# Issue order of one 1 MB output copy against the held weight loads in a top-2 expert layer

## The chip, the cores and the metric

One NeuronCore of a Trainium2 chip runs the whole program. The metric is the device time of one execution in microseconds (us). It was measured three times for the kernel before; the median is quoted. One further execution was recorded by the hardware profiler, and all rows of a profile come from that one.

In this document PE is the tensor engine, DVE the vector engine, ACT the scalar engine, POOL the GpSimd engine and SP the sync engine. SP computes nothing here: it issues DMAs, one after the other, in the order of the program. A q behind a name (SPq, POOLq) marks the instructions of that engine's sequencer.

## The reference

A residual layer with eight experts of three matrices each, of which every token uses two:

```python
var = jnp.mean(x * x, axis=-1, keepdims=True)
xn = rms_w * (x * jax.lax.rsqrt(var + EPS))
gate = xn @ wg_W + wg_b + (genre_embed @ gg_W + gg_b)
gate_w = jax.nn.softmax(gate, axis=-1)
topk_w, topk_i = jax.lax.top_k(gate_w, TOP_K)            # TOP_K = 2 of E = 8
cw = jnp.sum(jax.nn.one_hot(topk_i, E, dtype=x.dtype) * topk_w[..., None], axis=-2)
h1 = jax.nn.relu(jnp.einsum('bsh,ehm->bsem', x, W1) + b1)      # 256 -> 512
h2 = jax.nn.relu(jnp.einsum('bsem,emn->bsen', h1, W2) + b2)    # 512 -> 512
out_e = jnp.einsum('bsen,enh->bseh', h2, W3) + b3              # 512 -> 256
return jnp.einsum('bseh,bse->bsh', out_e, cw)
```

The result is `x + ref(x)`. `x` is 64 x 64 x 256 in float32, that is 4096 tokens of 1 KB each. An expert's W1 and W3 have 512 KB each and its W2 has 1 MB, so the weights make 16 MB and x makes 4 MB.

## The kernel before

The kernel does not compute all experts for all tokens. It computes the gate, sorts the 8192 (token, expert) pairs into tiles of 128 tokens that share an expert, gathers the rows of a tile, runs the three layers on them, and adds the weighted rows onto the output.

**Two parts.** Partition p holds the tokens 32p to 32p+31. The first NA = 8 columns of each partition (1024 tokens) are "the first part": their gate is computed first (`first_part`, L404), so that a first tile for each of the eight experts can start early. Tiles 0 to 7 hold rows of these tokens alone. The other 24 columns are routed while tiles 0 to 6 already run (`rest`, L556), and all later tiles come from that second table.

**The output** is built by addition. Plain copies put x into the output in DRAM, and each tile's weighted rows are then added to it by an indirect DMA (`give`, L862). The copies are `fills`. The first one (L509) covers the first 8 columns: 128 runs of 8 KB, 1 MB from DRAM to DRAM. Four more (L929) of 768 KB each follow during tiles 3 to 6. Each add waits for the add before it, the very first one waits for `fills[0]`, and the first add of the second table waits for the other fills.

**The order of the DMAs.** Everything is under a manual schedule, so each engine runs its instructions in program order. On SP this is: loads of x (L154), the bias vectors (L444 and L445), W1 and W2 of expert 0 (L395), and then what `other_loads` (L496) issues. Its first DMA is W3 of expert 0, and it carries an added dependence on `fetches[0]`, the gather of tile 0's 128 rows (`gather(0)`, L983). It is called the hold below. Since SP works in order, nothing behind the hold is issued until those rows have landed. Behind it come W1 of expert 1, b3 of experts 0 and 1, W2 and W3 of expert 1, the copy of the first columns (L509), the weights of expert 2, the rest of b3 and the weights of experts 3 to 7, in total some 15 MB besides the copy.

POOL issues the indirect DMAs: the gathers of rows into `xg` (L712), the gathers of the routing weights into `cg` (L712), the adds (L868), and it writes the routing weights to DRAM (L378).

PE transposes tile 0's rows (`transpose_x`, L767), ACT copies them to SBUF (L768), and then layer 1 (L831), layer 2 (L842) and layer 3 (L858) follow for each tile. ACT applies bias and relu (L834, L845), and DVE scales and adds the bias of the third layer (L867).

Of the kernel before, what the change touches and what calls it, by code (L numbers as in the profile page):

```python
# [21 lines left out]
def kernel(  # L22
# [17 lines left out]
    nc = tc.nc  # L40
# [13 lines left out]
    NA = 8  # L54
# [15 lines left out]
    xr = xrows.rearrange("(p i) h -> p i h", p=P)  # L70
    our = orows.rearrange("(p i) h -> p i h", p=P)
# [314 lines left out]
    fills, loads, fetches = [], [], []  # L386

    def load_weights(e, parts=(0, 1, 2)):
        for k in parts:
            dst, src = (  # L390
                (w1a[:, e], W1[e].rearrange("(p c) m -> p c m", c=HC)),
                (w2a[:, e], W2[e].rearrange("(c p) n -> p c n", p=P)),
                (w3a[:, e], W3[e].rearrange("(c p) h -> p c h", p=P)),
            )[k]
            loads.append(nc.sync.dma_start(dst, src))  # L395
# [100 lines left out]
    def other_loads():  # L496


        load_weights(0, (2,))
        tc.add_manual_dep(  # L500
            loads[2].ins,
            fetches[0].ins.name,
            mybir.DependencyInfo(mybir.DependencyClass.Sync, mybir.DependencyReason.DATA),
            reason="the first tile's rows go first",
        )
        load_weights(1, (0,))
        nc.sync.dma_start(b3_sb[:, 0:2], b3[0:2].unsqueeze(0).to_broadcast([P, 2, H]))
        load_weights(1, (1, 2))
        fills.append(nc.sync.dma_start(our[:, 0:NA, :], xr[:, 0:NA, :]))  # L509
        load_weights(2)  # L510
        nc.sync.dma_start(b3_sb[:, 2:E], b3[2:E].unsqueeze(0).to_broadcast([P, E - 2, H]))
        for e in range(3, E):
            load_weights(e)
# [467 lines left out]
    with tc.manual_schedule():  # L981
        first_part()
        gather(0)  # L983
        other_loads()
        gather(1)
        second_part()
# [73 lines left out]
```

## Time and profile before

| what | value |
|---|---|
| three executions | 511.5 to 511.92 us, median 511.85 us |
| the profiled execution | 513.2 us, of which its span is 511.4 us |
| granted PE clock, mean | 0.995 |
| PE busy | 495.6 us, 97% of the span |
| PE weight loads busy | 445.4 us, 87% |
| DVE / ACT / POOL busy | 239.2 / 167.3 / 288.9 us |
| HBM read / written | 42.80 / 20.71 MB |

The span is the stretch from the first to the last instruction in the profile. The page gives the busy time of each engine, the span in 40 slices, the DMA queues and the costliest groups of instructions. The trace behind it can be asked for the instructions of one engine in order of time, for what each engine waited for, and for the busy share of engines and DMA in any stretch. In such answers the first number of a timeline row is the start in us from the start of the span, the second the duration; square brackets tell how long the engine had been idle before the row and what ended that. A row of windows gives busy time and number of instructions of each engine, then the granted clock, the mean busy share of the 16 DMA engines, and the GB/s moved.

### The profile page before, as it was taken

The numbers are of one execution on the slowest core, as the hardware profiler recorded it, in microseconds if no ns is written. First come the engines' busy times: TensorE is split into PE (matmuls) and PEld (weight loads), VectorE is DVE, ScalarE is ACT, GpSimd is POOL, SyncE is SP. The second block draws the span as 40 slices with busy tenths as digits, with TensorE's granted clock in tenths as the row PEclk, the third lists the DMA queues.
The fourth block names the chain that finished last, engine by engine and source line by source line (L and its number), as shares of the span: only waits on it lengthen the run. The fifth ranks groups of instructions, "written<-read, shape, count | busy, mean of one in ns | idle before, by whom it ended". The sixth has DMA issues, their size and how long they took to land. (4 is left out here: it accounts for less than half of the span.)

```text
span 511.4 us, 8669 instructions
## 1 busy us (share of the span) xinstructions
PE 495.6 (97%) x2840; PEld 445.4 (87%) x2840; DVE 239.2 (47%) x587; ACT 167.3 (33%) x394; POOL 288.9 (56%) x229
## 2 busy tenths in 40 slices
PE   7899999999999999999999999999999999999992
PEld 6679999888888888888888888888888889999991
DVE  5895977244444334334333444443333335655550
ACT  5734444322222222222222222222222222444340
POOL 3455517766666656655556556666565545764621
PEclk9999999999999999999999999999999999999997
DMA  8699996454433343333433344433343333434201
GB/s 326 203 378 393 388 382 204 88 104 80 88 72 79 72 79 77 73 68 75 83 75 76 81 82 84 79 69 80 77 82 64 61 64 53 93 61 77 42 3 23
DMA packets 68257, 59.26 MB, mean 116 GB/s; under 512 B 39615, under 2 KB 59298, under 8 KB 67812
## 3 DMA queue, kind: packets, MB, share of 16 engines
q1 hardware_dynamic: 52608, 41.21, 24.6%
q0 software_dynamic: 15232, 17.34, 21.0%
q8 instruction: 25, 0.41, 0.3%
q14 instruction: 36, 0.29, 0.2%
q10 hardware_dynamic: 356, 0.01, 0.0%
HBM read 42.80 MB, written 20.71 MB: 124 GB/s over the span
## 5 line engine op out<-in xcount | busy, mean ns | idle before, releaser
L842 PE MATMUL pb<-hid,big 128*128 128x256 f32 (+1 forms) x1120 | 210.8, 346 | 0.0
L842 PEld LDWEIGHTS pb<-hid,big 128*128 128x128 f32 x1120 | 187.0, 191 | 20.4
L868 POOL DMA_INDIRECT out_dram<-y,idxR x59 | 97.8, 1658 | 127.9 <-issue 73.1
L845 ACT ACTIVATE hid<-pb,bb 128x256 f32<-128x256 f32 (+1 forms) x140 | 61.5, 440 | 245.7 <-PE pb L842 233.0
L797 DVE COPY big<-w2a 128x2048 f32 x35 | 44.7, 1278 | 160.4 <-PE pb L842 154.9
L831 PE MATMUL pb<-xT,big 128*128 128x256 f32 (+1 forms) x560 | 108.2, 346 | 0.0
L858 PE MATMUL pb<-big,hid 128*128 128x256 f32 x472 | 107.6, 379 | 0.0
L831 PEld LDWEIGHTS pb<-xT,big 128*128 128x128 f32 x560 | 93.5, 191 | 9.9
L858 PEld LDWEIGHTS pb<-big,hid 128*128 128x128 f32 x472 | 88.8, 190 | 11.6
L712 POOL DMA_INDIRECT big<-in_x_dram,idxR x59 | 78.8, 1336 | 20.7 <-issue 17.1
L712 POOL DMA_INDIRECT cg<-cwdR,idxR x59 | 69.0, 1169 | 18.0 <-issue 18.0
L834 ACT ACTIVATE hid<-pb,bb 128x256 f32<-128x256 f32 (+1 forms) x140 | 61.5, 440 | 40.9 <-PE pb L831 26.9
L867 DVE SCALAR_TENSOR_TENSOR y<-pb,cw,bc 128x256 f32<-128x256 f32 x59 | 28.5, 483 | 46.6 <-issue 26.2
L792 DVE COPY big<-w1a 128x1024 f32 x35 | 24.3, 695 | 25.5 <-PE pb L831 22.9
L842 PEld LDWEIGHTS pb<-hid,w2a 128*128 128x128 f32 x256 | 29.9, 192 | 2.3 <-issue 2.0
L842 PE MATMUL pb<-hid,w2a 128*128 128x128 f32 x256 | 30.7, 277 | 0.9 <-issue 0.9
L868 POOL DMA_INDIRECT out_dram<-y,idxA x8 | 15.7, 1963 | 25.1 <-DVE denB L370 7.8
L801 DVE COPY big<-w3a 128x1024 f32 x35 | 25.8, 737 | 2.8 <-issue 2.8
L816 DVE TENSOR_SCALAR bc<-b_sb,cw 128x256 f32 x59 | 22.9, 389 | 2.1
L756 DVE STREAM_TRANSPOSE xT<-gTs 128x256 f32<-128x256 f32 x57 | 22.5, 424 | 0.7 <-DMA gTs<-scr 0.7
L845 ACT ACTIVATE hid<-pb,vT 128x128 f32<-128x128 f32 x32 | 11.4, 367 | 25.3 <-PE pb L842 23.7
L831 PE MATMUL pb<-xT,w1a 128*128 128x128 f32 x128 | 16.0, 278 | 0.0
(224 smaller groups left out, 252.2 us busy)
## 6 DMA issues: line engine op xcount, KB each, us to landing
w2a<-in_L_cond_W_dram SPq DMA_DIRECT2D x8, 1024.0 KB
scr<-big SPq DMA_DIRECT2D x57, 128.0 KB
gTs<-scr SPq DMA_DIRECT2D x228, 32.0 KB
w1a<-in_L_cond_W_dram SPq DMA_DIRECT2D x8, 512.0 KB
w3a<-in_L_cond_W_dram SPq DMA_DIRECT2D x8, 512.0 KB
out_dram<-in_x_dram SPq DMA_DIRECT2D x4, 768.0 KB
big<-in_x_dram SPq DMA_DIRECT2D x4, 512.0 KB
big<-in_x_dram SPq DMA_DIRECT2D x2, 1024.0 KB
```

The source lines that it names most:

```text
L712: return nc.gpsimd.indirect_dma_start(out=dst, out_offset=None, in_=src, in_offset=bass.IndirectOffsetOnAxis(ap=index(b), axis=0), bounds_ ...
L792: V.tensor_copy(st1, w1a[:, e].rearrange("p e c m -> p (e c) m"))
L797: V.tensor_copy(st2, w2a[:, ex[u]].rearrange("p e c m -> p (e c) m"))
L801: V.tensor_copy(st3, w3a[:, ex[u]].rearrange("p e c m -> p (e c) m"))
L816: V.tensor_scalar(bc, b3e, cw, None, ALU.mult)
L831: nc.tensor.matmul(ph, lhsT=w1[:, c, ts(m, P)], rhs=cols[:, c, :], start=(c == 0), stop=(c == HC - 1))
L834: nc.scalar.activation(hids[:, 0, m, 0 : w * BT], ph, AF.Relu, bias=bb[:, 0, m : m + 1])
L842: nc.tensor.matmul(ph, lhsT=w2[:, m, ts(n, P)], rhs=hids[:, 0, m, 0 : w * BT], start=(m == 0), stop=(m == MC - 1))
L845: nc.scalar.activation(hids[:, 1, n, 0 : w * BT], ph, AF.Relu, bias=bb[:, 1, n : n + 1])
L858: nc.tensor.matmul(po, lhsT=hids[:, 1, n, ts(k, BT)], rhs=w3[:, n, :], start=(n == 0), stop=(n == MC - 1))
L867: V.scalar_tensor_tensor(y, sums(b), cw, bc, ALU.mult, ALU.add)
L868: add = nc.gpsimd.indirect_dma_start(out=orows, out_offset=bass.IndirectOffsetOnAxis(ap=index(b), axis=0), in_=y, in_offset=None, bounds_c ...
```

## The change

The copy of the first eight columns is issued as the first DMA of `other_loads`, ahead of the hold, and no longer behind W3 of expert 1. Nothing else differs: the same DMAs with the same sizes are issued, on the same queue, and the dependences are the same.

```diff
     def other_loads():
 
 
+        fills.append(nc.sync.dma_start(our[:, 0:NA, :], xr[:, 0:NA, :]))
         load_weights(0, (2,))
         tc.add_manual_dep(
             loads[2].ins,
...
         load_weights(1, (0,))
         nc.sync.dma_start(b3_sb[:, 0:2], b3[0:2].unsqueeze(0).to_broadcast([P, 2, H]))
         load_weights(1, (1, 2))
-        fills.append(nc.sync.dma_start(our[:, 0:NA, :], xr[:, 0:NA, :]))
         load_weights(2)
         nc.sync.dma_start(b3_sb[:, 2:E], b3[2:E].unsqueeze(0).to_broadcast([P, E - 2, H]))
```

## The prediction

> **What bounds the kernel now.** I read the busy times of the page first, then the list of what PE waited for after the first 20 us, because PE is the engine that is never free.
>
> ```profile
> PE 495.6 (97%) x2840; PEld 445.4 (87%) x2840; DVE 239.2 (47%) x587; ACT 167.3 (33%) x394; POOL 288.9 (56%) x229
> DMA  8699996454433343333433344433343333434201
> ```
> ```profile
> PE pb L842 <- issue: 0.9, 1, 0.9
> PE pb L767 <- DMA xg<-in_x_dram,idxA: 0.7, 1, 0.7
> ```
>
> PE is at 97%. From 20 to 505 us it has two idle moments. In one (0.7 us, at 22.00) it waits for the rows of tile 0, in the other (0.9 us, at 36.77) for no weight: layer 2 of tile 1 needs ACT's last relu of layer 1, which ends at 37.67. PE never waits for a weight load. So a PE instruction that starts later at 22 us ends the kernel later by as much, and a weight that lands earlier is worth nothing. The DMA row shows full rings (9) only in the slices up to 77 us, and a dip in the second. The timelines of SP, PE and POOL show what happens in the dip:
>
> ```profile
> 11.55 0.43 SPq L395 DMA_DIRECT2D w2a<-in_L_cond_W_dram  x1
> 21.98 0.37 SPq L395 DMA_DIRECT2D w3a<-in_L_cond_W_dram  x1
> 24.95 0.68 SPq L509 DMA_DIRECT2D out_dram<-in_x_dram  x1
> ```
> ```profile
> 20.22 1.06 PE L214 MATMUL pb<-hid,wg_sb 128*32 128x512 f32 x8
> 22.00 0.50 PE L767 MATMUL pb<-ident,xg 128*128 128x128 f32 x2 [0.72 <-DMA xg<-in_x_dram,idxA]
> ```
> ```profile
> 19.04 1.12 POOL L712 DMA_INDIRECT xg<-in_x_dram,idxA  x1 [6.12 <-DVE denA L369]
> 23.17 0.63 POOL L378 DMA_DIRECT2D cwdA<-cw8A  x1 [0.29 <-POOL cw8A L377]
> 30.07 1.06 POOL L712 DMA_INDIRECT cg<-cwdA,idxA  x1 [3.62 <-DMA cwdA<-cw8A]
> ```
>
> SP stands at the hold from 12 to 21.98. The gather of tile 0 leaves POOL at 19.04+1.12 = 20.16, and PE has its rows at 22.00: 1.84 us. What the rings do meanwhile is in the windows (the last two numbers: DMA share, GB/s):
>
> ```profile
> 17.00:18.00 1.00, 0.99 (x13) 0.98 (x14) 0.88 (x3) 0.90 (x2) 0.00 (x0) 1.00 0.64 242
> 18.00:19.00 1.00, 1.00 (x12) 0.83 (x11) 0.54 (x5) 0.00 (x0) 0.00 (x0) 1.00 0.07 18
> 19.00:20.00 1.00, 1.00 (x9) 0.93 (x9) 0.90 (x6) 0.59 (x1) 0.96 (x1) 1.00 0.00 0
> 20.00:21.00 1.00, 1.00 (x11) 0.21 (x9) 0.93 (x5) 0.58 (x1) 0.69 (x2) 1.00 0.18 41
> 33.00:34.00 1.00, 1.00 (x11) 1.00 (x10) 0.90 (x6) 0.40 (x2) 0.83 (x1) 1.00 1.02 425
> 34.00:35.00 1.00, 1.00 (x7) 0.90 (x7) 0.83 (x6) 0.06 (x1) 0.87 (x1) 1.00 1.04 438
> ```
>
> The loads ahead of the hold run out between 17 and 18. In windows of a quarter us the rings carry nothing from 18.5 to 20.75, where the packets of the gather begin; they end at 21.5.
>
> **The change part by part.** It removes and adds no instruction. It moves one SP issue (0.68 us by its row) from 24.95 to about 12.0, where SP would only wait, so that issue costs nothing and the hold still ends with the gather. Behind the hold five DMAs keep their place, and everything from W1 of expert 2 on is issued without the 0.7 us and without the copy's data in the rings. If that cover (the hold) were gone, the 0.68 us would fall on SP, which PE does not wait for.
>
> How long does the copy take in the rings? The packet records show 8 KB packets, which only this transfer has in that stretch, from 32.6 to 35.4, of 309 ns each, eight to an engine: 8 x 0.309 = 2.47 us. The windows above agree: 1.05 MB at 425 to 438 GB/s are 2.4 to 2.5 us. How much room is there? Until 20.75 the free share is 0.36 + 0.93 + 1.00 + 0.75 = 3.04 us of all 16 engines. So on the mean engine the copy ends some 0.5 us before the gather's first packet. The last packets of the loads are over just after 18.0, so the slowest engine ends the copy at about 18.1 + 2.47 = 20.6, still 0.15 us before it. Two instruction fetches stand in the same hole (packets of 0.47 us at 17.9 and 1.07 us at 18.3); if one of them lands on a late engine, that engine ends at up to 21.6.
>
> What is late then is the gather of tile 0, and with it PE's transposes at 22.00, ACT's copy at 22.54, layer 1 at 22.97 and all of PE behind them, one for one. Call this delay d. It is bounded from both sides. Below: zero, because the index of the gather comes from DVE at 18.8 and nothing in the change touches that. Above: the same trace shows what a POOL transfer pays with the rings full. The write of the routing weights leaves POOL at 23.17+0.63 = 23.80 and its waiter goes on at 30.07, 6.3 us, where the gather in empty rings had 1.84. Fully loaded rings would therefore cost up to 4.4 us more. I take d = 0.2 us, near the empty case, because by the sum the copy has gone on nearly all engines.
>
> Here two rules of the Trainium skill speak. "DMA: Bandwidth & Descriptors", in the section on the anatomy of one DMA, fits a transfer as about 2.0 us fixed plus its bytes at 436 GB/s. For the copy that makes 2.0 + 2.4 = 4.4 us, ending at 17.6 + 4.4 = 22.0 instead of 20.1, and would put it right on the gather (an estimate of d = 22.0 - 20.75 = 1.25, which gives 513.1). The packet rows show 2.47 us back to back in the rings, since the fixed part is latency and occupies no engine, so I use the row. The same page, on queues and rings, says that an engine takes turns between its queues packet by packet. Then a leftover of the copy would cost each of the gather's two packets per engine one packet of 0.31 us, d = 0.6 at most (512.45). The row of 6.3 us does not look like fair turns, so the trace leaves more room than the rule. I use the rule for the middle and the row for the tail.
>
> What is gained? The weights and b3 behind the copy's old place land about 2.5 us earlier. W1 of expert 2 is needed at 40.7 and its bytes pass at about 36, so it was early already: nothing. The last fills and the first gathers of the second table meet freer rings near 80 us, and PE does not wait there either: nothing. The add that waits for this copy starts at 42.23 after a DVE wait: nothing. One thing could be positive. ACT's relus of layer 1 of tile 1 run 1 us apart (33.69, 35.13, 35.87, 37.30) instead of the 0.45 of tile 0, just while the copy's packets pass, and PE's 0.95 us of idleness follows from it. If the copy caused that, up to 0.95 us comes back. The fills of 768 KB later, also from DRAM to DRAM, show no such gap, so I count 0.
>
> **The sum.** Profiled execution: span 511.4 + 0.2 = 511.6, and with the 1.8 us around it 513.2 + 0.2 = 513.4. The median of the runs is 1.35 us under the profiled execution; the same difference on it gives 511.85 + 0.2 = 512.05, told as 512.0.
>
> **The rivals.**
> (1) Hidden, as summed: 512.0, chance 0.67. For it: the 3.04 us of room against 2.47. Against it: the margin is only 0.15 to 0.5 us, and the copy writes DRAM as well.
> (2) Slower: the copy's tail is still in the rings when POOL hands over the gather. It decides from the point where an engine still holds copy packets after about 20.7. Place: tile 0's rows at 22.00. Price: an engine with the long fetch ends at 21.6; if the gather's first packet then still needs the 0.6 us that it needs in empty rings (20.16 to 20.75), it starts at 22.2, so d is 22.2 - 20.75 = 1.45, hence 513.3; with the full queueing of the 6.3 us row d = 4.4, 516.3. Chance of d over 1 us: 0.25.
> (3) Faster: the copy was what spread ACT's relus at 33 to 37 us. The gain is 0.95 us of PE's idleness and no more, since PE has no other; 510.9, with a little more if the timed runs lose more there. For it: the coincidence in time. Against it: the lag begins before the copy's first packet, and the timed runs are 1.35 us under the profiled one, so they may not have it at all. Chance of more than 0.2%: 0.08.
> (4) The copy is hidden in both places, so that only noise moves. This lies inside case (1).
>
> **How the numbers follow.** 0.2% of 511.85 is 1.0 us, about what a measurement of this kernel can tell from no change. Within it lies case (1), with d up to 1.0, and most of a recovered 0.95: 0.67. Slower is case (2), 0.25, faster what is left of case (3), 0.08. The range reaches from the full recovery, 510.9, to the 513.3 of case (2); beyond it I leave about 0.07 below and 0.12 above, for longer queueing.
>
> **What would show it.** Right: the copy's SP row at about 12.0; DMA shares near 1 in the windows 17 to 20 and falling before 21; SP's hold ending within 0.3 us of 21.98; PE's L767 row near 22.0; later SP rows some 2.5 us earlier once rings limit them. Case (2): L767 at 23 or later, and its idle time, ended by the DMA of xg, up from 0.72 by as much as the end moves. Case (3): the four relus of L834 for tile 1 some 0.45 us apart and no idle row of L842 at 37.7. I am wrong if the gather, though handed to nearly empty rings, lands over 1 us late, or if PE waits somewhere new behind 38 us.

## The result and the profile after

In 20 executions of each kernel the changed one has a median of 512.8 us, the one before 511.93 us. The ratio is 1.0018, with a 95% interval from 1.001 to 1.0025: slower by 0.9 us, between 0.5 and 1.3. A second comparison, in the last set of runs below, gave 1.0019 (1.0011 to 1.0027). A third, on a chip where executions of one kernel spread over 8 us, gave 0.9969 (0.9941 to 0.9998), that is, the other way. The profiled execution took 513.64 us, with a span of 511.8 us.

The busy times and the DMA slices of the page after follow. They look like those of before, except that the rings (the queues of the 16 DMA engines) are fuller in the second slice (7 in place of 6) and emptier in the seventh (4 in place of 6):

```profile
PE 495.4 (97%) x2840; PEld 445.5 (87%) x2840; DVE 238.2 (47%) x587; ACT 167.6 (33%) x394; POOL 290.1 (57%) x229
DMA  8799994454433344333443344334433333433201
```

What PE waited for, of the changed kernel (engine, line, what ended the wait; us in total, times, longest):

```profile
PE pb L767 <- DMA xg<-in_x_dram,idxA: 1.4, 1, 1.4
PE pb L767 <- DMA big<-in_x_dram,idxR: 0.9, 1, 0.9
```

The wait for tile 0's rows has doubled, from 0.7 to 1.4 us. The idle row of L842 is gone, and a new wait has come: the rows of tile 9, one of the first two tiles of the second table. SP's timeline after:

```profile
11.60 0.43 SPq L395 DMA_DIRECT2D w2a<-in_L_cond_W_dram  x1
12.07 0.68 SPq L499 DMA_DIRECT2D out_dram<-in_x_dram  x1
22.71 0.39 SPq L395 DMA_DIRECT2D w3a<-in_L_cond_W_dram  x1
```

The copy is issued at 12.07, as meant. The hold ends at 22.71, 0.73 us later than before. POOL's and PE's timelines after:

```profile
19.07 1.12 POOL L712 DMA_INDIRECT xg<-in_x_dram,idxA  x1 [6.11 <-DVE denA L369]
23.19 0.63 POOL L378 DMA_DIRECT2D cwdA<-cw8A  x1 [0.29 <-POOL cw8A L377]
29.10 0.99 POOL L712 DMA_INDIRECT cg<-cwdA,idxA  x1 [2.51 <-DMA cwdA<-cw8A]
```
```profile
20.25 1.07 PE L214 MATMUL pb<-hid,wg_sb 128*32 128x512 f32 x8
22.74 0.50 PE L767 MATMUL pb<-ident,xg 128*128 128x128 f32 x2 [1.42 <-DMA xg<-in_x_dram,idxA]
```

POOL hands over tile 0's gather at 19.07 + 1.12 = 20.19, as early as before (20.16). PE has the rows 2.55 us after that, where it was 1.84. The windows after (last two numbers: DMA share and GB/s):

```profile
17.00:18.00 1.00, 0.96 (x13) 0.96 (x13) 0.91 (x3) 0.94 (x2) 0.00 (x0) 1.00 1.08 365
18.00:19.00 1.00, 1.00 (x11) 0.86 (x10) 0.53 (x4) 0.00 (x0) 0.00 (x0) 1.00 1.10 457
19.00:20.00 1.00, 1.00 (x9) 0.91 (x9) 0.88 (x6) 0.59 (x1) 0.93 (x1) 1.00 0.97 410
20.00:21.00 1.00, 1.00 (x11) 0.24 (x9) 0.93 (x5) 0.59 (x1) 0.69 (x2) 1.00 0.55 205
```

The hole is filled. The copy thins out from 20.0 on, and its last 8 KB packet runs from 20.80 to 21.11. The records of tile 0's landing tell the rest. The semaphore of the gather is counted up 16 times, which I take as one count for each of the 16 DMA engines. Before, the recorded counts (11 of the 16) lie between 21.62 and 21.96. After, 15 of them lie between 21.70 and 22.22, and the last comes at 22.69. The packet records show what stood in the way. Before, PE's next block of instructions (one packet of 16 KB, 1.07 us) was fetched at 18.33, in the empty hole. After, the same fetch begins at 20.52 and ends at 21.48. The two packets of the gather that end last start at 21.47 and 21.90.

**The two profiled executions, added up.** After tile 7's layer 2 starts (L842 at 86.28 before, 86.73 after) both need 425.1 us, so all of the difference lies ahead of it. Up to PE's first transpose of tile 0 the changed kernel loses 0.74 us. From there to tile 7's layer 2 PE needs 62.81 us where nothing holds it up (so, within 0.03, in five of the profiles below). Before it took 64.28, because ACT's relus of layer 1 of tile 1 came late and L842 waited for them (called the slow layer 1 of tile 1 from here on); after it took 63.99, because of the wait for tile 9's rows. That wait came again with half the copy ahead (0.9 us) and with the copy one step later, but in neither of the other two profiles of the changed kernel. The sum 0.74 - 0.29 = 0.45 is the difference of the spans (511.4 and 511.8). It is half of the 0.9 us of the timed runs, and it mixes in two events of which each profile has one that the other lacks.

### The profile page after: what moved, and what is told of

Its sections match the earlier page's. It is cut to its first block, busy times and chain, and to the rows that moved or that the text cites. A ratio compares the mean times of both kernels' runs of the same rounds, so it can differ in the third digit from the quotient of the medians.

```text
span 511.8 us, 8669 instructions
## 1 busy us (share of the span) xinstructions
PE 495.4 (97%) x2840; PEld 445.5 (87%) x2840; DVE 238.2 (47%) x587; ACT 167.6 (33%) x394; POOL 290.1 (57%) x229
## 5 line engine op out<-in xcount | busy, mean ns | idle before, releaser
L842 PE MATMUL pb<-hid,big 128*128 128x256 f32 (+1 forms) x1120 | 210.8, 347 | 0.0
L842 PEld LDWEIGHTS pb<-hid,big 128*128 128x128 f32 x1120 | 187.1, 191 | 20.2
L831 PE MATMUL pb<-xT,big 128*128 128x256 f32 (+1 forms) x560 | 108.3, 347 | 0.0
L831 PEld LDWEIGHTS pb<-xT,big 128*128 128x128 f32 x560 | 93.6, 191 | 9.8
L712 POOL DMA_INDIRECT big<-in_x_dram,idxR x59 | 80.9, 1371 | 20.9 <-issue 16.8
L842 PEld LDWEIGHTS pb<-hid,w2a 128*128 128x128 f32 x256 | 29.7, 192 | 1.1 <-issue 0.8
L842 PE MATMUL pb<-hid,w2a 128*128 128x128 f32 x256 | 30.3, 276 | 0.0
L816 DVE TENSOR_SCALAR bc<-b_sb,cw 128x256 f32 x59 | 23.3, 395 | 2.1
L831 PE MATMUL pb<-xT,w1a 128*128 128x128 f32 x128 | 15.9, 278 | 0.0
## 6 DMA issues: line engine op xcount, KB each, us to landing
w1a<-in_L_cond_W_dram SPq DMA_DIRECT2D x8, 512.0 KB, 11.7
w3a<-in_L_cond_W_dram SPq DMA_DIRECT2D x8, 512.0 KB, 13.1
big<-in_x_dram SPq DMA_DIRECT2D x4, 512.0 KB, 4.2
```

The costliest lines, as they stand in the source:

```text
L712: return nc.gpsimd.indirect_dma_start(out=dst, out_offset=None, in_=src, in_offset=bass.IndirectOffsetOnAxis(ap=index(b), axis=0), bounds_ ...
L816: V.tensor_scalar(bc, b3e, cw, None, ALU.mult)
L831: nc.tensor.matmul(ph, lhsT=w1[:, c, ts(m, P)], rhs=cols[:, c, :], start=(c == 0), stop=(c == HC - 1))
L842: nc.tensor.matmul(ph, lhsT=w2[:, m, ts(n, P)], rhs=hids[:, 0, m, 0 : w * BT], start=(m == 0), stop=(m == MC - 1))
```

## The experiments

Theory 1: whatever is still in the rings when POOL hands over tile 0's gather delays it, and the end with it. The rivals, which the expectations number 2 to 5 (not the numbers of the prediction's own rivals), were that moving the issue costs in itself, that the copy's DRAM writes slow the gather, that the engines take fair turns between queues, and that the old place had a cost of its own. For each profile I give the time from the end of the POOL row of that gather (the hand-over) to PE's first transpose, called the hand-over time. POOL hands over between 19.4 and 21.8 us in these executions. With empty rings the hand-over time is the same all along, 1.85 us at 19.83 and 1.83 us at 21.35. With the copy ahead it can also depend on how early POOL comes.

**Half of the copy ahead.**

```diff
+        fills.append(nc.sync.dma_start(our[:, 0 : NA // 2, :], xr[:, 0 : NA // 2, :]))
         load_weights(0, (2,))
...
-        fills.append(nc.sync.dma_start(our[:, 0:NA, :], xr[:, 0:NA, :]))
+        halves.append(nc.sync.dma_start(our[:, NA // 2 : NA, :], xr[:, NA // 2 : NA, :]))
...
-            behind = [adds[-1]] if adds else [fills[0]]
+            behind = [adds[-1]] if adds else [fills[0], *halves]
```

> Half of the copy (columns 0 to 3, 0.52 MB) ahead of the hold, the other half at the old place. Theory 1 (what is still in the rings when tile 0's gather is handed over delays it, one for one to the end): the half copy ends near 18.1 + 1.24 = 19.3 us, a PE instruction fetch of 1 us behind it near 20.3, before the gather's packets at 20.9; PE's L767 row stays at 22.0 and the time is that of before (511.9 to 512.1). Rival 2 (the moved issue itself, or what follows behind the hold, costs): about half of the measured +0.87 us, so 512.4.

Ratio 1.0001 (0.9989 to 1.0013): no loss that can be seen, as theory 1 has it. But the interval is too wide to exclude that the half costs 0.5 us, as the second rival has it. The one profile is not as expected: 2.39 us from the hand-over (18.61 + 1.12) to the first transpose at 22.12, so that L767 stood near 22.0 only because POOL was early. This profile separates the copy from the fetch. The half copy was over at 19.90, before the gather's first packet (20.43), and 15 engines had landed by 21.56, 1.83 us after the hand-over, as in empty rings. The instruction fetch ran from 19.90 to 20.86, the last two packets of the gather started at 20.89 and 21.35, and the 16th engine landed at 22.07, 0.51 us behind all others.

**Plain loads ahead in place of the copy.**

```diff
         load_weights(0, (2,))
+        load_weights(1, (0,))
+        held = nc.sync.dma_start(b3_sb[:, 0:2], b3[0:2].unsqueeze(0).to_broadcast([P, 2, H]))
         tc.add_manual_dep(
-            loads[2].ins,
+            held.ins,
...
-        load_weights(1, (0,))
-        nc.sync.dma_start(b3_sb[:, 0:2], b3[0:2].unsqueeze(0).to_broadcast([P, 2, H]))
```

> The copy stays at its old place; instead W3 of expert 0 and W1 of expert 1 (1.05 MB of plain loads) are issued ahead of the hold, which now sits on the load of b3. Theory 1: any megabyte ahead of the hold fills the hole in the same way, L767 at about 22.7 and the time 512.6 to 512.9. Rival 3 (it is the copy's writes to DRAM that slow the gather): L767 at 22.0 and 511.9 to 512.1.

Ratio 1.0022 (1.0012 to 1.0032), and the profile, POOL and PE rows:

```profile
18.76 1.12 POOL L712 DMA_INDIRECT xg<-in_x_dram,idxA  x1 [6.11 <-DVE denA L369]
22.33 0.50 PE L767 MATMUL pb<-ident,xg 128*128 128x128 f32 x2 [1.33 <-DMA xg<-in_x_dram,idxA]
```

22.33 - 19.88 = 2.45 us. A megabyte of loads into SBUF costs about what the megabyte of copy costs, so the loss needs neither the DRAM writes nor anything else of the copy, and the rival of the DRAM writes falls. Here no single engine was late: the loads ran on until 21.46, and the last count (22.28) came only 0.19 us behind the one before it.

**More ahead: the copy and one later fill, 1.84 MB.**

```diff
+        fills.append(nc.sync.dma_start(our[:, 0:NA, :], xr[:, 0:NA, :]))
+        fills.append(nc.sync.dma_start(our[:, NA : NA + NB // NF, :], xr[:, NA : NA + NB // NF, :]))
         load_weights(0, (2,))
...
-        fills.append(nc.sync.dma_start(our[:, 0:NA, :], xr[:, 0:NA, :]))
...
-        if u >= E - 1 - NF:
+        if u > E - 1 - NF:
```

> The copy and the first of the later fills (0.79 MB more) ahead of the hold, three fills left at their place. Theory 1 with the rings served in the order of arrival: the rings are full until 20.5 + 1.86 = 22.4, the gather's packets end behind them, L767 near 24.2 to 24.6, 2.2 to 2.6 us later than before, and the time 514 to 514.5. Rival 4 (each engine takes turns between its queues packet by packet): two packets of the gather per engine wait 0.31 us each, so L767 not later than 22.9 and 512.7 to 513.0.

Ratio 1.0065 (1.0044 to 1.0086), 3.3 us. POOL hands over at 19.46 + 1.12 = 20.58; PE and the windows of this profile (the third number from the end is the granted clock; the edit shifts the lines by two, so L769 and L833 are L767 and L831 of before):

```profile
24.17 0.51 PE L769 MATMUL pb<-ident,xg 128*128 128x128 f32 x2 [2.47 <-DMA xg<-in_x_dram,idxA]
25.14 3.30 PE L833 MATMUL pb<-xT,w1a 128*128 128x128 f32 x16
```
```profile
21.00:22.00 1.00, 0.70 (x8) 0.00 (x0) 0.93 (x5) 0.64 (x2) 1.00 (x1) 1.00 1.05 416
22.00:23.00 1.00, 0.00 (x0) 0.00 (x0) 0.68 (x4) 0.31 (x1) 0.90 (x4) 1.00 0.80 287
...
26.00:27.00 1.00, 1.00 (x7) 1.00 (x7) 0.93 (x5) 0.57 (x2) 1.00 (x1) 0.50 0.74 244
27.00:28.00 1.00, 1.00 (x6) 1.00 (x6) 0.61 (x4) 0.45 (x2) 0.69 (x2) 0.50 1.11 391
28.00:29.00 1.00, 1.00 (x7) 1.00 (x6) 0.00 (x0) 0.42 (x2) 0.69 (x2) 0.50 1.05 426
```

Two things are seen. The first transpose comes 3.59 us after the hand-over, at 24.17, where service in the order of arrival had put it (24.2 to 24.6). Fair turns allowed 22.9, or 23.3 with POOL 0.42 us later than before; six of the 16 engines landed later than that, so the rival of fair turns falls. And after 2.47 us without work PE is given half its clock from 25.7 to 29.1 us: layer 1 of tile 0 takes 3.30 us instead of the 2.05 of the kernels before and after, and PE reaches layer 2 of tile 0 1.65 us late. Together 1.75 + 1.65 = 3.4 us, near the measured 3.3 (2.3 to 4.4). The half clock was not in the profiled execution alone: four of the six timed ones have a mean granted clock of 0.989 or 0.990, against 4 of 43 of the kernel before.

**No first copy.** The first eight columns of the output are not filled with x.

```diff
-        fills.append(nc.sync.dma_start(our[:, 0:NA, :], xr[:, 0:NA, :]))
...
-            behind = [adds[-1]] if adds else [fills[0]]
+            behind = [adds[-1]] if adds else []
```

> The first copy is left out, so the first 8 columns of each partition are not filled with x before the adds; everything else as before. Theory 1: the copy was hidden at its old place, 511.9 to 512.1. Rival 5 (at the old place the copy's packets spread ACT's relus of tile 1 at 33 to 37 us, and PE lost 0.95 us there): about 0.95 us faster, 511.0, with the relus of L834 for tile 1 0.45 us apart and no idle PE row at 37.7.

Ratio 0.9998 (0.9987 to 1.0009); once more, on another chip:

> The first copy left out once more (the first 8 columns of each partition are not filled with x before the adds). Theory 2: no slow layer 1 of tile 1 in the profile, and where the kernel before shows it often, faster than before by more than 0.1%. Theory 0: 1.000.

1.0005 (0.9996 to 1.0014). Both profiles hand over in 1.83 and 1.88 us, without a slow layer 1 of tile 1. At its old place the copy costs nothing that can be measured, so no other place for it can be expected to gain more than some 0.1%.

**The two kernels once more, for what repeats.** No edit.

> The kernel before, profiled once more, to see what of its profile repeats. Theory 1: from the hand-over of tile 0's gather (end of its POOL row) to PE's first transpose 1.8 us again. The slow layer 1 of tile 1 (relus 1 us apart, PE idle 0.95 us at 36.8) was an accident of one execution, since it was absent in the three other profiles that keep the copy, or half of it, at its old place or leave it out: expected absent here, and PE from the first transpose to layer 2 of tile 7 (L842) in 62.8 us, or 63.9 us if tile 8's rows come late. Time 511.9 to 512.2, ratio 1.000.

> The changed kernel, profiled once more. Theory 1: 2.4 to 2.6 us from hand-over to the first transpose, 0.6 to 0.75 more than before; ratio 1.0010 to 1.0025.

On the chip of this set, executions of one and the same kernel lay between 512 and 520 us, so its ratios (0.9994, interval 0.9964 to 1.0023, for the kernel before against itself; 0.9969, 0.9941 to 0.9998, for the changed one) say little on 0.2%. Most of the spread goes with PE's clock: of 67 executions of the kernel before, the 43 with a mean granted clock up to 0.991 have a median of 518.3 us, the other 24 one of 513.7; of the changed kernel, 9 of 21 are of the first kind, and the other 12 have a median of 513.65. The profiles tell more. Before: hand-over at 19.83, first transpose at 21.68, 1.85 us. After: 19.53 and 22.27, 2.74 us. But the slow layer 1 of tile 1, which I expected to be absent, was there again in the kernel before (2.15 us lost). So a last set, on a quieter chip:

> The kernel before, profiled a third time. So far the slow layer 1 of tile 1 (PE over 1 us late between layer 2 of tile 1 and layer 1 of tile 2) was in 3 of 4 profiles with the whole copy at its old place, and in none of the profiles without it. Theory 2 (the copy's packets, passing at 32 to 35 us, hold up what ACT waits for): again 1.4 us or more lost between 13.8 and 18.7 us after PE's first transpose. Theory 0 (an accident of single executions): lost or not, at random. Ratio 1.000.

> The changed kernel, profiled a third time, on the same chip as the three others of this set. Theory 1 with theory 2: hand-over to first transpose 2.4 to 2.75 us (0.6 to 0.9 over before), no slow layer 1 of tile 1. Ratio 1.001 to 1.0025 on a chip like those of the first two comparisons; under 1.000 on one where the kernel before loses more to the slow layer 1, as on the chip of the second set, where this kernel came out at 0.9969.

The changed kernel came out at 1.0019 (1.0011 to 1.0027), the kernel before against itself at 1.0004 (0.9993 to 1.0016). The changed kernel's rows:

```profile
18.30 1.12 POOL L712 DMA_INDIRECT xg<-in_x_dram,idxA  x1 [6.13 <-DVE denA L369]
22.19 0.50 PE L767 MATMUL pb<-ident,xg 128*128 128x128 f32 x2 [1.65 <-DMA xg<-in_x_dram,idxA]
```

22.19 - 19.42 = 2.77 us. In the kernel before, PE itself was late this time, because it had half its clock from 20.73 to 24.14 us. Eight matmuls that took 1.09 us in the first profile of this kernel took 1.69 (its timeline row, then a row of its windows):

```profile
20.39 1.69 PE L196 MATMUL pb<-ident,big 128*128 128x128 f32 x8
```
```profile
22.00:23.00 1.00, 1.00 (x9) 0.20 (x8) 0.93 (x5) 0.64 (x2) 0.97 (x2) 0.50 0.47 131
```

Tile 0's rows landed 1.80 us after the hand-over, and layer 1 of tile 1 was not slow, although the copy was at its old place.

**The copy one step later.**

```diff
-        fills.append(nc.sync.dma_start(our[:, 0:NA, :], xr[:, 0:NA, :]))
         load_weights(2)
+        fills.append(nc.sync.dma_start(our[:, 0:NA, :], xr[:, 0:NA, :]))
```

> The copy one step later than before, behind the three weights of expert 2 instead of ahead of them, so that its packets pass at about 37.5 to 40.5 us. Theory 2: the slow stretch moves with it, and the relus of tile 1's layer 1 at 33 to 36 us are 0.45 us apart, while layer 2 of tile 1 or layer 1 of tile 2 is slow instead. Theory 0: the slow stretch, if there is one, stays at 32 to 38 us. Hand-over to first transpose 1.85 us either way; ratio 0.999 to 1.002.

Hand-over 1.77 us; no slow layer 1 of tile 1 and no slow stretch elsewhere; PE waited 0.9 us for tile 9's rows. Ratio 1.002 (1.0003 to 1.0036), so later is not better. Its cause was not looked for. A ratio of 1.002 alone does not point to a late gather, then: here the gather was on time. Part of it may be PE's clock, since six of its 22 executions have a mean granted clock up to 0.991, against three of 67 of the kernel before.

**PE's instruction fetch earlier.** The changed kernel with 13 more small matmuls ahead:

```diff
-        busy(7)
+        tiny(10)
+        busy(5)
...
         for _ in chosen:
             pass
+        tiny(3)
         pA.ranks()
...
+    def tiny(n):
+
+        for _ in range(n):
+            nc.tensor.matmul(PB[7][:, 256:264], lhsT=ones, rhs=ones[:, 0:8], start=True, stop=True)
```

> The changed kernel with 13 small matmuls on PE more (10 before the warm-up transposes, of which 2 go, and 3 in the gap before the rank matmuls), so that PE reaches its next block of instructions some 2 us earlier and asks for it at about 16 us instead of 18.3. Theory 1a (the last of the 16 engines serves PE's 16 KB instruction fetch after the copy and before the gather): the fetch is served earlier, by 19.5, the last engine no longer lags, and the hand-over to first transpose takes 2.1 us instead of 2.55; ratio to the kernel before 1.0005 to 1.001. Theory 1b (the copy's own tail alone, in all engines): still 2.4 to 2.6 us, ratio 1.0015 to 1.002.

A miss as a test: ratio 1.0028 (0.9999 to 1.0057), on the chip with the wide spread. The fetch did move, to 18.77. But the matmuls delayed the hand-over to 21.75, and the loads of x ahead of the copy ended later too: on the slowest engine at 21.21, where it was 18.66 in the changed kernel. The fetch now stood among these loads. The copy's own packets on that engine ran until 23.66 (21.21 + 2.47 = 23.68), the last two of the gather started at 23.66 and 23.82, and the last count came 0.38 us behind the one before it. So one engine was late all the same, perhaps since it kept the delay of the fetch while the rings were full; the records do not name it, and theory 1a is not tested. PE's rows:

```profile
24.42 0.50 PE L774 MATMUL pb<-ident,xg 128*128 128x128 f32 x2 [1.54 <-DMA xg<-in_x_dram,idxA]
25.39 3.48 PE L838 MATMUL pb<-xT,w1a 128*128 128x128 f32 x16
```

The first transpose came 2.67 us after the hand-over. Layer 1 of tile 0 took 3.48 us, again at half the clock (from 25.75 to 29.16 us), after an idle time of only 1.54 us.

**Two gathers ahead of an add.** The kernel before, with the gathers of tiles 8 and 9 put ahead of tile 4's add on POOL:

```diff
         for b in range(E, E + 4):
             gather(b)
+            if b == E + 1:
+                add_rows(*put_off.pop())
...
+            if u == 4:
+                put_off.append((b, y))
+            else:
+                add_rows(b, y)
```

> The kernel before, with the first two gathers of the second table (tiles 8 and 9) put ahead of tile 4's add on POOL, which waits some 7.8 us for the add before it to land. If the wait for tile 8's rows at 85 us (0.9 us in the profile of the changed kernel) is the second thing that sets the time, it is gone here: PE from the first transpose to layer 2 of tile 7 always in 62.8 us, ratio 0.998 to 0.9995. If it is rare in unprofiled runs, 1.000. If tile 4's later add then holds tile 5's add and the rows behind it, over 1.001.

1.0006 (0.9971 to 1.0042) on the uneven chip: open. In its profile there was no wait for the rows of tiles 8 and 9, but layer 1 of tile 1 lost 6.6 us, with PE at half its clock from 38.69 to 45.52 us, so that PE came late anyway.

## Why the prediction was right or wrong

The forecast was 512.0 with a range of 510.9 to 513.3, and no change clear of noise as the likeliest. Measured were 512.8 and a loss of 0.18%, inside the range and, by its middle, just under 0.2%, but on the slow side: the interval (0.10 to 0.25%) leaves out no change and takes in part of rival 2. That it fell within case (1) is in part luck, because the delay was four times the one that was summed. The hand-over time by profile, and how far the last of the gather's counts came behind the one before it, as recorded:

| ahead of the hold | hand-over to first transpose | last count behind the one before | ratio to before |
|---|---|---|---|
| nothing (before, three profiles without a late PE) | 1.84, 1.85, 1.85 us | 0.04, 0.02, 0.04 us | |
| nothing, no copy at all | 1.88, 1.83 us | 0.06, 0.02 us | 0.9998, 1.0005 |
| half the copy | 2.39 us | 0.51 us | 1.0001 |
| 1.05 MB of loads | 2.45 us | 0.19 us | 1.0022 |
| the copy (after, three profiles) | 2.55, 2.74, 2.77 us | 0.47, 0.61, 0.42 us | 1.0018, 1.0019 |
| 1.84 MB | 3.59 us | 0.26 us | 1.0065 |

The third value of the first row is from the kernel with the two gathers ahead of an add, where nothing near tile 0 is changed. Told from the start of the span, PE's first transpose lies at 22.00, 21.68 and 22.27 in these three and at 22.74, 22.27 and 22.19 in the changed kernel: POOL happened to hand over earlier in two of the latter, and only the hand-over time shows the delay clearly.

**What bounds the kernel** was right: PE needs the same 425.1 us from tile 7's layer 2 to the end in both kernels, so what is lost at tile 0 is lost at the end, unless a later wait takes it up.

**The gains counted at nothing** were nothing: without any copy the ratio is 1.000, within 0.15%.

**The time of the copy in the rings**, 2.47 us by its packets, was right for most engines: 13 of 16 had ended by 20.80. For the slowest engine the sum had 20.6; it ended at 21.11, and at 21.44 and 21.38 in the other two profiles, though POOL handed over 0.7 us earlier there. The sum let the loads ahead of the copy end on every engine by 18.1, as before; on the slowest engine they now ended at 18.66. At the old place, too, the copy's packets lie between 32.69 and 35.99, wider than the prediction's 32.6 to 35.4; and a row of windows books a packet where it starts, so that the rings seem to carry nothing from 18.5 on, although the fetch ran until 19.40. The formula of the Trainium skill ("DMA: Bandwidth & Descriptors", anatomy of one DMA: a fixed part plus bytes), which the page fits to transfers issued by POOL, while SP issues this copy, would have put its end at 22.0 when taken as a time for which the rings are taken. No packet of the copy ran that long.

**The term that was mis-sized is d.** I took 0.2 us "because by the sum the copy has gone on nearly all engines". On nearly all it had. But PE goes on when the last of 16 engines has counted, and with the copy ahead the last engine was, as far as the records show, the one that also served an instruction fetch of 1 us. I had named the fetch, and that its engine "ends at up to 21.6" (21.48 was recorded), and then put it into the tail of the range instead of the middle. Against the mean of before, d is 0.71, 0.90 and 0.93 us in the three profiles, mean 0.84. That this is close to the 0.9 us of the timed runs is no proof of its own, because the two other events (the slow layer 1 of tile 1 and the wait for tile 9's rows) are left out of it. PE's clock is not the reason of the loss: among the executions of the last set with a mean granted clock of 0.992 or more, the medians are still 512.64 and 512.01 us.

Of d, 0.47, 0.61 and 0.42 us are the one engine behind all others; without it d would have been 0.24, 0.29 and 0.51 us, not far from the prediction's 0.2 in two of the three. The records do not name engines, but they leave little choice. In the second profile no packet of the copy is in flight from 20.61 to 20.77, only the fetch (19.81 to 20.78); as it ends, one last packet of the copy runs until 21.44, and the last two packets of the gather start at 21.44 and 21.60. The third has the same order (fetch until 20.72, the copy's last packet until 21.38, the gather's last two from 21.38 and 21.53). With half the copy the fetch was the only thing in the way. Where the fetch ran in empty rings, no engine was behind by more than 0.06 us. No run moved the fetch away and left the rest alone, so this stays an inference; and with the loads and with 1.84 MB ahead, most of the delay was the tail of the bytes themselves.

**The rule that I used for the middle**, turns between queues packet by packet, does not hold here for the gather. With 1.84 MB ahead it came 1.75 us late and not the 0.6 us of two packets' turns. Its first packet, which starts 0.70 us after the hand-over in empty rings, started 1.37 us after it, when the first engine had finished its share of the bytes. The row of the full rings (6.3 us) should have had more weight. In the profile after, the same transfer took 29.10 - 23.82 = 5.3 us.

**Rival 2** was the nearest, with its place, its hand-over and its fetch; only its price was too high (1.45 us for 0.7 to 0.9). **Rival 3** (of the prediction) supposed that the copy at its old place spreads ACT's relus. In the five profiles of kernels with the whole copy at the old place, layer 1 of tile 1 was slow in three; in the other nine nothing of the kind was seen. But leaving the copy out gains nothing, and one of the five is the kernel before itself (its profile on the quieter chip), with nothing slow. What makes layer 1 of tile 1 slow at times stays open.

## What to carry to other kernels

An idle stretch of the DMA rings ahead of a small transfer that an engine waits for is not free room: what fills it must be gone from the slowest of the 16 engines, with the instruction fetches that it pushes back, before the small transfer is handed over. Reckon with the slowest engine, not the mean one, leave a margin of more than one such fetch (1 us here), or put the bulk transfer where nothing is waited for. A profile that differs from another by one event of 1 us is no measure of an effect of 1 us: compare the stretch in question over several profiles, from one event to the next.

## What the runs showed of the hardware

**A small transfer waits for most of what was issued ahead of it.** With 1.05 MB issued 7 us earlier a 128 KB gather from POOL took 0.6 to 0.9 us longer to land, with 1.84 MB 1.75 us longer, whether the bytes went to SBUF or to DRAM. The order of arrival is not strict: in two of the changed kernel's profiles one packet of the copy was served after the instruction fetch, although SP had issued the copy as early as 11.4 and 11.3 us and the fetch was served at 19.8.

**A fetch of PE instructions takes about 1 us of one DMA engine** (16 KB, 0.96 to 1.07 us in the kernels before and after of the first comparison, up to 1.39 us elsewhere). That it is PE's is read from the counts: in the profile before, PE starts some 250 matmuls and weight loads between two such fetches, the other engines far fewer instructions. In a full ring it started 2.2 us later (20.52 instead of 18.33) without PE stopping for it.

**Half a clock came without a long idle time.** The granted clock fell to 0.50 for 3.41 us after 2.47 us without work (1.84 MB ahead, a cost of 1.65 us), after 1.54 us (the earlier fetch, 1.64 us), and in one profile of the kernel before, in which PE had no idle time above 0.16 us in the 4.8 us ahead. The 1.42 to 1.65 us of idleness in the changed kernel's three profiles left it at 1.00. So the length of one idle time does not decide it here; what does stays open. The Trainium skill, "TensorE: Matmul & The Clock Gate", in its part on the clock gate, gives an idle window of about 3.4 us as what it takes; no idle time here was that long.
